# One list of 143 slot tiles for both parts of a grouped FFN, with its loads, prelude and last gathers rearranged

## The chip, the cores and the metric

The kernel runs on one core of a Trainium2 chip. The core has five engines with instruction streams of their own: TensorE (PE in the profile, with PEld for its weight loads), VectorE (DVE), ScalarE (ACT), GpSimd (POOL) and SyncE (SP, which issues transfers here). Sixteen DMA engines move data between HBM and the core's memory. The metric is the device time of one execution in microseconds (us); lower is better.

## The reference

Six residual blocks on 4096 tokens of width 256 (8 sequences of 512), each after a layer norm:

```python
x = x + 0.5 * L0_ffn(layernorm(x))     # 8 experts, each takes its best 1024 tokens, FF = 1024
x = x + L0_attn(layernorm(x))          # 16 heads of 16, rope, causal
x = x + 0.5 * L0_ffn(layernorm(x))
x = x + 0.5 * L1_ffn(layernorm(x))     # the grouped FFN of this case
x = x + L1_attn(layernorm(x))          # 16 heads of 64, no mask
x = x + 0.5 * L1_ffn(layernorm(x))     # the grouped FFN again, same weights
```

The block of this case routes every token to 4 of 16 experts and adds a shared expert:

```python
scores = softmax(xt @ gate_w.T)                     # 16 experts in 4 groups
gmask  = the 2 groups with the largest maximum
indices = top 4 of the masked scores; weights = scores at indices
a = silu(x @ w1[e]) * (x @ w3[e])                   # 256 -> 128 for each chosen expert e
y = sum over chosen e of weights[e] * (a @ w2[e])   # 128 -> 256
z = (silu(xt @ ws1) * (xt @ ws3)) @ ws2             # shared expert, inner width 256
return y + z
```

## The kernel before, in words

The residual x stays in the core's memory as 32 tiles of 128 tokens (`TT`). The blocks run one after the other: `ffn0(0)`, `attn0`, `ffn0(1)`, `ffn1_before` (the first grouped FFN), `attn1`, `ffn1_after` (the second). Inside the grouped FFNs every engine executes in the order in which the code is written; nothing is rearranged.

A grouped FFN works through lists in HBM. For each token and each of its four experts, `routing` computes a slot: a row in `slots_d`. The rows of one expert stand together and begin on a multiple of 128, so that a tile of 128 slots has one expert (`owner`). `send` scatters the normed rows of a token tile into their slots with four indirect DMAs from GpSimd (L1250). `tile_steps` then runs over the slot tiles, two at a time: `load` fetches a pair into one of four `xs` buffers from SP's queue (L1511), `turn` transposes it (tpx), `hide` multiplies with the expert's w1 and w3 (hs), `back` transposes the activations (tpa), and `give` multiplies with w2 (yps) and writes the result to `ys_d` (L1566). The stages of neighbouring pairs are interleaved: step i does `hide` of i - 2, `back` of i - 3, `turn` of i and `give` of i - 4. Slots that no token fills are zero rows; `clear` writes them once, in `ffn0(0)`.

`gather` brings the four result rows of each token of a tile back (L1357, four indirect DMAs from GpSimd, `yg` with two buffers), and `add` adds them to x on VectorE, weighted (L1370). `collect` makes a list of such steps: step t adds what step t - 2 gathered, and gathers for t. The number in `flying` says how many gathers may be under way: a gather waits for the one that many places before it. Sends have two under way.

The tokens are split in two parts with lists of their own (`PARTS`): 12 and 20 token tiles in the first grouped FFN, 20 and 12 in the second. A list for t token tiles must hold `slot_tiles(t)` slot tiles in the worst case, since each expert may leave one tile partly filled: 63 for 12 and 95 for 20. So part 0 can be sent and worked on while part 1 is still being routed, and part 0's results are gathered while part 1's tiles are in the loop.

- In `ffn1_before` the norms, logits and routing of part 0 come first, then its sends, then those of part 1, and beside them the shared expert's work as units in a `Pump` (`hidden` units with four matmuls, `outputs` units with two; while routing runs, the pump does one unit after every two or three steps of routing). After that come the 80 loop steps. From five steps after the last pair of part 0 one in three loop steps also does a step of `collect` for part 0. The weights of `attn1` (4 MB) are loaded from SP's queue at that point.
- In `attn1` part 1 is gathered in small pieces between the attention's work, and part 0 of the second FFN is normed, routed (`Front`) and sent.
- In `ffn1_after` part 1 is normed and its logits computed, then the loop starts; each of its first steps also does four steps of part 1's routing. Here two in three steps collect part 0 from the same point on. After the loop, 48 units of the shared expert run, and after every second unit one collecting step, first what is left of part 0 (two gathers under way), then part 1 (four).

`load(j)` is issued by `turn(j - 4)`, and each load waits for all sends of its part. Since SP works in order, a load that waits holds back the writes of `ys` behind it.

Of the kernel before, what the change touches and what calls it, by code (L numbers as in the profile page):

```python
# [19 lines left out]
P = 128  # L20
# [25 lines left out]
PARTS = 12, 20  # L46
# [9 lines left out]


def slot_tiles(t):

    return (t * P * TOPK + E1 * (P - 1)) // P  # L60


class Kernel:
    def __init__(self, ctx, tc, w):
# [59 lines left out]
        self.slots_d, self.ys_d = {}, {}  # L124
        for t in PARTS:
            self.slots_d[t] = self.dram.tile([slot_tiles(t) * P, D], F32, name=f"slots_d{t}")
            self.ys_d[t] = self.dram.tile([slot_tiles(t) * P, D], F32, name=f"ys_d{t}")

    def clear(self, zero, part, parts):

        for t in PARTS:
            rows = self.slots_d[t].rearrange("(j p) d -> p j d", p=P)
            a, b = slot_tiles(t) * part // parts, slot_tiles(t) * (part + 1) // parts
            self.nc.sync.dma_start(out=rows[:, a:b, :], in_=bc(zero, 1, b - a))
# [777 lines left out]
    def _attn1(self, ctx, weights, one, after):  # L912
# [191 lines left out]
        def listed(n):  # L1104
            b, c = divmod(n, NC)
            got = gathered(n - 1) if 1 <= n <= one.parts[1] + 2 else []
            if c == 0:
                ranges = []
                if b == 0:
                    ranges.append((self.stats1, QT, 2 * QT))  # L1110
                elif 2 <= b < B - 1:
                    got += [each(means, self.stats1, (b + 1) * QT + i) for i in range(0, QT, 2)]
                    ranges.append((self.stats1, (b + 1) * QT, QT))
# [106 lines left out]
class Grouped:  # L1220


    def __init__(self, k, n, parts):
        self.k, self.n, self.parts = k, n, parts
        self.base = (0, parts[0])
        self.tiles = [slot_tiles(t) for t in parts]
        self.slots_d = [k.slots_d[t] for t in parts]
        self.ys_d = [k.ys_d[t] for t in parts]
        late, most = k.late, max(parts)
# [4 lines left out]
        self.owner = [late.tile([1, slot_tiles(most)], I32, name=f"owner{h}") for h in range(2)]  # L1234
# [10 lines left out]
    def send(self, h, t, row):  # L1245

        nc, tc = self.k.nc, self.k.tc
        key = f"slots{self.n}{h}"
        for r in range(TOPK):
            inst = nc.gpsimd.indirect_dma_start(  # L1250
                out=self.slots_d[h][:, :],
                out_offset=bass.IndirectOffsetOnAxis(ap=self.slot[h][:, r, t : t + 1], axis=0),
                in_=row, in_offset=None,
                bounds_check=self.tiles[h] * P - 1, oob_is_err=True,
            ).ins
            before = self.sent[-2:-1]
            for other in before:
                tc.add_manual_dep(inst, other.name, SYNC, reason="two transfers at a time")
            tc.declare_no_dep(inst, group=key, keep=before, reason="slots of one part are all different")
# [4 lines left out]
    def routing(self, h, lg, pool, row_psum):  # L1264
# [49 lines left out]
        tiles_i = pool.tile([P, E1], I32, name="tiles_i")  # L1314
        nc.vector.tensor_scalar(tiles_i, inc[:, :, HT - 1], float(P - 1), None, ALU.add)
        nc.vector.tensor_scalar(tiles_i, tiles_i, 7, None, ALU.arith_shift_right)
        nc.vector.tensor_tensor(inc.rearrange(flat), inc.rearrange(flat), pb, ALU.subtract)
        pa = row_psum(E1 * HT)
        nc.tensor.matmul(pa, lhsT=k.tri, rhs=chosen.rearrange(flat), start=True, stop=True)
        tiles = pool.tile([P, E1], F32, name="tiles")  # L1320
        nc.vector.tensor_copy(tiles, tiles_i)
        upto = pool.tile([P, E1], F32, name="upto")
        nc.vector.tensor_tensor_scan(upto, k.ones[:, 0:E1], tiles, 0.0, ALU.mult, ALU.add)
        base = pool.tile([P, E1], F32, name="base")
        nc.vector.tensor_tensor(base, upto, tiles, ALU.subtract)
        nc.vector.tensor_scalar(base, base, float(P), None, ALU.mult)
        nc.vector.tensor_tensor(inc.rearrange(flat), inc.rearrange(flat), pa, ALU.add)
        yield
        nc.vector.tensor_tensor(inc, inc, bc(base, 2, HT), ALU.add)
# [11 lines left out]
        past = pool.tile([P, E1], F32, name="past")  # L1341
        number = pool.tile([P, 1], F32, name="number")
        nc.vector.tensor_scalar(past, upto, k.lanes[:, 0:1], None, ALU.is_le, ALU.add, accum_out=number)  # L1343
# [8 lines left out]
    def gather(self, h, t, flying):  # L1352

        nc, tc = self.k.nc, self.k.tc
        y = self.y[h, t] = self.k.late.tile([P, TOPK, D], F32, name="yg", bufs=2)
        for r in range(TOPK):
            inst = nc.gpsimd.indirect_dma_start(  # L1357
                out=y[:, r, :], out_offset=None, in_=self.ys_d[h][:, :],
                in_offset=bass.IndirectOffsetOnAxis(ap=self.slot[h][:, r, t : t + 1], axis=0),
                bounds_check=self.tiles[h] * P - 1, oob_is_err=True,  # L1360
            ).ins
            for other in self.got[-flying : 1 - flying]:
                tc.add_manual_dep(inst, other.name, SYNC, reason="few transfers at a time")
            self.got.append(inst)

    def add(self, h, t, ranks=range(TOPK)):
        at = self.base[h] + t
        x = self.k.x[:, at, :]
        for r in ranks:
            self.k.nc.vector.scalar_tensor_tensor(  # L1370
                x, self.y[h, t][:, r, :], self.coef[h][:, r, t : t + 1], x, ALU.mult, ALU.add
            )

    def collect(self, h, flying, then=None):

        def step(t):
            def run():
                if t >= 2:
                    self.add(h, t - 2)
                    if then is not None:  # L1380
                        then(self.base[h] + t - 2)
                if t < self.parts[h]:
                    self.gather(h, t, flying)
            return run
        return [step(t) for t in range(self.parts[h] + 2)]
# [66 lines left out]
    def shared(self, g):  # L1452
# [4 lines left out]
        def hidden(s):  # L1457
# [14 lines left out]

            def dve():
# [4 lines left out]
        def outputs(i):  # L1478
# [11 lines left out]

            def dve():
# [6 lines left out]
    def tile_steps(self):  # L1498
# [3 lines left out]
        where = [(h, i, min(2, self.tiles[h] - i)) for h in range(2) for i in range(0, self.tiles[h], 2)]  # L1502
        st = [{} for _ in where]

        def load(j):

            if j >= len(where):
# [3 lines left out]
            inst = nc.sync.dma_start(  # L1511
                out=st[j]["xs"][:, :n, :],
                in_=self.slots_d[h].rearrange("(j p) d -> p j d", p=P)[:, i : i + n, :],
            ).ins
            for other in self.of_part[h]:
                tc.add_manual_dep(inst, other.name, SYNC, reason="all rows of the part are there")

        def turn(j):
            h, i, n = where[j]
# [10 lines left out]
            load(j + 4)  # L1530
# [24 lines left out]
        def give(j):  # L1555
            h, i, n = where[j]
            yp = psum.tile([P, 2, D], F32, name="yps", tag="y", bufs=2)
            for u in range(n):
# [7 lines left out]
            nc.sync.dma_start(  # L1566
                out=self.ys_d[h].rearrange("(j p) d -> p j d", p=P)[:, i : i + n, :], in_=ys[:, :n, :]
            )
# [5 lines left out]

        first = sum(h == 0 for h, _, _ in where)
        return load, step, len(where) + 4, first


# [27 lines left out]


def ffn1_before(k, f):
# [3 lines left out]
    with ExitStack() as ctx, k.tc.manual_schedule(engines={E.PE, E.DVE, E.Activation, E.Pool, E.SP}):  # L1612
# [15 lines left out]
        f.logits(2, lg, 2 * QT)  # L1628
# [4 lines left out]
        pump.feed(groups[0][0] + groups[1][0] + groups[0][1] + groups[2][0])  # L1633
        steps = f.routing(0, lg, f.route, f.row_psum)
        pump.run(1)
        more = True
        while more:
            more = advance(steps, 3)
            pump.run(1)
        for t in range(a):  # L1640
            f.send(0, t, f.xn[:, t, :])
        load, step, total, first = f.tile_steps()
# [4 lines left out]
        k.ln_range(f.route, f.stats, a, 8)  # L1647
        pump.feed(groups[1][1] + groups[2][1])
        pump.run(2)
        f.normal(3)  # L1650
        f.normal(4)
        pump.run(2)
        f.columns(3)
        k.ln_range(f.route, f.stats, a + 8, TT - a - 8)
        pump.run(2)
        f.columns(4)
        f.logits(3, lg, 0)
        for g in range(5, 8):
            f.normal(g)
            pump.run(2)  # L1660
        pump.run(len(pump.units))
        f.logits(4, lg, QT)
        pump.feed(groups[3][0])
        for g in range(5, 8):
            f.columns(g)
            pump.run(1)
            f.logits(g, lg, (g - 3) * QT)
        pump.feed(groups[4][0] + groups[3][1])
        for g in range(5, 8):
# [245 lines left out]
```

## Time and profile before

| | |
|---|---|
| timed runs | 4051.42 us median of three (4050.55 to 4054.75) |
| profiled execution | 4017.39 us, span 4015.7 us, mean granted TensorE clock 0.936 |
| busy in the span | PE 3662.2 us (91%), DVE 1858.5 (46%), ACT 1432.8 (36%), POOL 1203.8 (30%) |
| first grouped FFN | x is back at 1859.06 us, first slot tile transposed at 2029.18, attention's first transposes at 2310.58 |
| second grouped FFN | first norm operation at 3560.73, first slot tile transposed at 3581.12, first gather of part 0 at 3763.31, last gather at 3980.06 |

The profile shows one execution on the core. "Busy" is the time in which an engine executes instructions; a wait is given with what ended it. A group "yg<-ys_d" is the instructions that write the tile yg from ys_d, and "L1357" is the line that issued them. Times within the span are counted from its start.

### The profile page before, as it was taken

What the parts mean: (1) busy time and instruction counts of PE and PEld (TensorE: products, weight loads), DVE (VectorE), ACT (ScalarE), POOL (GpSimd) and SP (SyncE); (2) the same over time, 40 slices, a digit from 0 to 9 for tenths busy, and PEclk for the clock granted to TensorE, in tenths of its full rate; (3) what the DMA queues carried; (4) which work ended last, traced back from release to release, by engine and by line L of the source; (5) the groups of instructions that cost most, each with busy time, mean ns of one, the idle gap of its engine ahead of it and who ended that gap; (6) DMA issues with size and microseconds to landing.
All of it is one profiled execution on the core that took longest, in us unless ns stands there. A gap on an engine that the chain in (4) does not pass through costs nothing.

```text
span 4015.7 us, 52125 instructions
## 1 busy us (share of the span) xinstructions
PE 3662.2 (91%) x18444; PEld 2343.5 (58%) x18444; DVE 1858.5 (46%) x4396; ACT 1432.8 (36%) x2849; POOL 1203.8 (30%) x1074
## 2 busy tenths in 40 slices
PE   5799995999997599997798999999999999989978
PEld 5466662555556366665487845555555554558855
DVE  5312206555553421213733556666556576554444
ACT  2122221444443122222122355555455554533311
POOL 2233335334322133331553322220000004504254
PEclk6899997999986599998899999999999999989989
DMA  8533322010103033324256600110000001136543
GB/s 271 161 73 75 73 30 80 17 27 17 28 22 106 18 77 71 70 52 123 78 198 218 188 28 27 30 29 1 1 1 1 1 1 48 58 108 218 182 147 105
DMA packets 256141, 306.99 MB, mean 76 GB/s; under 512 B 34320, under 2 KB 225936, under 8 KB 255632
## 3 DMA queue, kind: packets, MB, share of 16 engines
q1 hardware_dynamic: 206736, 202.43, 15.8%
q0 software_dynamic: 49152, 101.24, 10.5%
q8 instruction: 153, 2.51, 0.3%
q14 instruction: 100, 0.82, 0.1%
HBM read 161.48 MB, written 133.69 MB: 74 GB/s over the span
## 4 chain that ended last, share of the span: by engine, by line
PE 41%; issue 4%; DVE 3%; DMA 3%; POOL 3%; ACT 1%; POOLq 0%; DVEq 0%; ACTq 0%; SPq 0%
PE sp L986 6%; PE tp L1006 6%; PE zp L1033 6%; PE pq L964 6%; PE hs L1537 4%; PE yp L1048 3%; PE pv L953 3%; PE yps L1559 2%; POOL slots_d L1250 2%; DMA yg<-ys_d,slot 2%; PE hp L1464 2%; POOL yg L1357 1%; PE tpx L1523 1%; DMA acc_d<-ob,idx 1%; PE rp L1020 1%
## 5 line engine op out<-in xcount | busy, mean ns | idle before, releaser
L478 PE MATMUL hp<-exT,w 128*128 128x512 f32 x1024 | 453.4, 597 | 0.0
L492 PE MATMUL op<-w,hid 128*128 128x256 f32 x2048 | 451.9, 380 | 0.0
L995 ACT ACTIVATE ex<-sp,nmax 128x512 f32<-128x512 f32 x512 | 344.7, 685 | 242.3 <-DVE nmax L992 242.3
L492 PEld LDWEIGHTS op<-w,hid 128*128 128x128 f32 x2048 | 387.7, 190 | 64.3 <-issue 15.3
L1357 POOL DMA_INDIRECT yg<-ys_d,slot x256 | 266.0, 1039 | 510.2 <-DVE x L1370 296.2
L497 DVE TENSOR_TENSOR ob<-op,b 128x256 f32<-128x256 f32 x128 | 54.4, 425 | 647.4 <-PE op L492 572.0
L731 DVE CUSTOM_DVE_ANT_0 junk<-sp,mask 128x128 f32<-128x128 f32 (+3 forms) x512 | 251.1, 490 | 198.0 <-PE sp L722 174.3
L499 POOL DMA_INDIRECT acc_d<-ob,idx x128 | 207.1, 1618 | 439.8 <-ACT ob L498 193.0
L992 DVE TENSOR_REDUCE nmax<-sp 128x2 f32<-128x1024 f32 x256 | 301.7, 1220 | 80.3 <-PE sp L986 80.2
L478 PEld LDWEIGHTS hp<-exT,w 128*128 128x128 f32 x1024 | 193.5, 191 | 219.9 <-issue 216.9
L1006 PEld LDWEIGHTS tp<-ident,ex 128*128 128x128 f32 x2048 | 234.4, 141 | 147.4 <-issue 86.6
L1537 PE MATMUL hs<-w_sb,xT 128*128 x1264 | 310.4, 390 | 2.5 <-DMA xs<-slots_d 1.3
L482 ACT ACTIVATE hid<-hp,b 128x512 f32<-128x512 f32 x256 | 175.9, 687 | 342.3 <-PE hp L478 342.3
L1006 PE MATMUL tp<-ident,ex 128*128 128x128 f32 x2048 | 272.5, 275 | 6.7 <-ACT ex L995 5.4
L1537 PEld LDWEIGHTS hs<-w_sb,xT 128*128 128x128 f32 x1264 | 248.4, 197 | 39.2 <-ACT xT L195 2.7
L1250 POOL DMA_INDIRECT slots_d<-wide,slot x176 | 174.4, 991 | 318.3 <-DVE past L1343 144.3
L986 PE MATMUL sp<-qk,qk 64*128 64x512 f32 x1024 | 254.4, 615 | 0.0
L964 PE MATMUL pq<-xnT,wide 128*128 128x512 f32 x512 | 247.5, 607 | 1.2 <-ACT xnT L195 0.8
L197 DVE COPY eT<-tp 128x512 f32<-128x512 f32 x256 | 176.9, 691 | 140.7 <-PE tp L1006 139.9
L1033 PE MATMUL zp<-eT,v 128*64 128x512 f32 x1024 | 236.0, 603 | 0.0
L195 ACT COPY eT<-tp 128x512 f32<-128x512 f32 x256 | 149.5, 584 | 240.4 <-PE tp L1006 240.4
L449 POOL DMA_INDIRECT ex<-xn_d,idx x128 | 131.3, 1025 | 345.9 <-DVE idx L440 311.8
(298 smaller groups left out, 5512.3 us busy)
## 6 DMA issues: line engine op xcount, KB each, us to landing
xs<-slots_d SPq DMA_DIRECT2D x156, 256.0 KB, 2.8
ys_d<-ys SPq DMA_DIRECT2D x156, 256.0 KB, 2.5
w<-in_W SPq DMA_DIRECT2D x32, 1024.0 KB, 6.1
w_sb<-in_w SPq DMA_DIRECT2D x24, 512.0 KB, 6.5
slots_d<-zero SPq DMA_DIRECT2D x7, 1536.0 KB, 12.9
xn_d<-xn SPq DMA_DIRECT2D x16, 512.0 KB, 4.2
acc_d<-x SPq DMA_DIRECT2D x8, 1024.0 KB, 5.7
x<-acc_d SPq DMA_DIRECT2D x8, 1024.0 KB, 9.5
```

Of the source, the lines that this page charges most:

```text
L478: nc.tensor.matmul(hp, lhsT=w1[:, c, f * P : f * P + P], rhs=exT[e][:, c, h * CH : h * CH + CH], start=(c == 0), stop=(c == DC - 1),)
L492: nc.tensor.matmul(op, lhsT=hid[h][:, f, i * P : i * P + P], rhs=w2[:, f, :], start=(f == 0), stop=(f == FC - 1),)
L731: nc.vector.tensor_tensor_reduce(out=junk[:, :wd], in0=sps[h // 2][:, h % 2, at : at + wd], in1=mask[:, S - wd :], scale=1.0, scalar=NEG, ...
L964: nc.tensor.matmul(pp, lhsT=(wq, wk)[a][:, k, c * P : c * P + P], rhs=xnT[b][:, k, :], start=(k == 0), stop=(k == DC - 1),)
L986: nc.tensor.matmul(sp[:, j, :], lhsT=q[r, qt * P : qt * P + P], rhs=k[r, :], start=True, stop=True)
L992: nc.vector.tensor_reduce(nmax, sp, AX.X, ALU.max, negate=True)
L995: nc.scalar.activation(ex[:, j, :], sp[:, j, :], AF.Exp, bias=nmax[:, j : j + 1], accum_out=ch["sums"][:, qt, j : j + 1],)
L1006: nc.tensor.transpose(tp[:, k, :], ch["ex", qt][:, j, k * P : k * P + P], self.ident)
L1033: nc.tensor.matmul(zp[DK1 * j : DK1 * j + DK1, :], lhsT=v[b, h][:, k, at : at + DK1], rhs=ch["eT"][:, j, k, :], start=(k == 0), stop=(k == ...
L1250: inst = nc.gpsimd.indirect_dma_start(out=self.slots_d[h][:, :], out_offset=bass.IndirectOffsetOnAxis(ap=self.slot[h][:, r, t : t + 1], ax ...
L1357: inst = nc.gpsimd.indirect_dma_start(out=y[:, r, :], out_offset=None, in_=self.ys_d[h][:, :], in_offset=bass.IndirectOffsetOnAxis(ap=self ...
L1537: nc.tensor.matmul(hp[:, u].rearrange("p a i -> p (a i)"), lhsT=st[j]["xT"][:, u, c, :], rhs=self.w13[:, bass.ds(st[j]["e"][u], 1), c, :]. ...
```

## The change

Both parts now share one list. Part 0 fills whole tiles from the front: of the rows of an expert, those that make full tiles go to that expert's tiles (`upto`), and the rest, fewer than 128, go to one tile per expert behind them (`tail`), which part 1 completes before it opens new tiles. In all there are `SLOT_TILES` = 143 tiles. The first 4a - 16 of them (a token tiles in part 0) are full for certain once part 0 is sent, so they are what `tile_steps` calls the tiles of h = 0: 48 in the first FFN, whose parts are now 16 and 16, and 64 in the second (20 and 12). All others (95 and 79) wait for both parts. Part 0's results stand in the first 4a + 16 tiles (`whole`), and its gathers may start when those are written: 40 and 48 pairs (`known`).

- The loads of the tiles of h = 1 are issued when the loop reaches them, four at once and then one ahead by four as before; in the last four steps of h = 0 nothing is loaded.
- Sends have four under way instead of two.
- In `ffn1_before` the norms, columns and logits of part 1 become steps of a generator, followed by its routing, and `Pump.beside` runs units beside both routings: three steps for a hidden unit, one for an output unit, four when there is no unit.
- Collecting beside the loop: three in five steps in both FFNs (before: one in three, two in three). In `ffn1_after` routing takes three steps per loop step instead of four.
- After the loop of `ffn1_after` the collecting steps that are left are spread evenly over the units, and part 1 is gathered four token tiles deep: every second tile uses two `xs` buffers in place of a `yg`.

```diff
-PARTS = 12, 20
+PARTS = (16, 16), (20, 12)
+SLOT_TILES = (NT * TOPK + E1 * (P - 1)) // P
...
     def clear(self, zero, part, parts):
-        for t in PARTS:
-            rows = self.slots_d[t].rearrange("(j p) d -> p j d", p=P)
...
+        rows = self.slots_d.rearrange("(j p) d -> p j d", p=P)
+        a, b = SLOT_TILES * part // parts, SLOT_TILES * (part + 1) // parts
+        self.nc.sync.dma_start(out=rows[:, a:b, :], in_=bc(zero, 1, b - a))
...
+        first = TOPK * parts[0] - E1
+        self.starts, self.tiles = (0, first), (first, SLOT_TILES - first)
+        self.whole = TOPK * parts[0] + E1
...
     def send(self, h, t, row):
-            before = self.sent[-2:-1]
+            before = self.sent[-4:-3]
...
     def routing(self, h, lg, pool, row_psum):
+        if h == 0:
+            nc.vector.tensor_copy(tiles_i, count)
+            nc.vector.tensor_scalar(tiles_i, tiles_i, 7, None, ALU.arith_shift_right)
...
+            nc.vector.tensor_tensor(jump, tail, at, ALU.subtract)
...
+        nc.vector.scalar_tensor_tensor(beyond, inc, 0.0, bc(jump, 2, HT), ALU.is_ge, ALU.mult)
+        yield
+        nc.vector.tensor_tensor(inc, inc, bc(at, 2, HT), ALU.add)
+        nc.vector.tensor_tensor(inc, inc, beyond, ALU.add)
...
-    def gather(self, h, t, flying):
+    def gather(self, h, t, flying, more=False):
+        if more and t % 2:
+            halves = [self.work.tile([P, 2, D], F32, name="xs", bufs=4) for _ in range(2)]
+            y = [halves[r // 2][:, r % 2, :] for r in range(TOPK)]
...
-    def collect(self, h, flying, then=None):
+    def collect(self, h, flying, then=None, more=False):
+        depth = 4 if more else 2
...
         def turn(j):
+            if j == early:
+                for ahead in range(4):
+                    load(j + ahead)
...
-            load(j + 4)
+            if j >= early or j + 4 < early:
+                load(j + 4)
...
+    def beside(self, steps):
+        more = True
+        while more:
+            more = advance(steps, self.units[0][0].steps if self.units else 4)
+            self.run(1)
...
 def ffn1_before(k, f):
+        def second():
+            for g in range(a // QT, TT // QT):
+                for i in range(0, QT, 2):
+                    for t in range(g * QT + i, g * QT + i + 2):
+                        k.ln_mean(f.route, f.stats, t)
+                    yield
+                y = k.ln_root(f.route, f.stats, g * QT, QT)
+                yield
+                k.ln_rest(f.route, f.stats, g * QT, QT, y)
+                yield
+                f.normal(g)
+                yield
+                f.columns(g)
+                f.logits(g, lg, g * QT - a)
+                pump.feed(groups[g][0])
...
+            yield from f.routing(1, lg, f.route, f.row_psum)
+        pump.beside(second())
...
-        begin, weights = first + 5, None
+        begin, weights = known + 5, None
...
-            if i >= begin and (i - begin) % 3 == 0 and coming:
+            if i >= begin and (i - begin) % 5 % 2 == 0 and coming:
...
 def ffn1_after(k, f, out):
-        begin = first + 5
+        begin = known + 5
...
-                sending = not advance(steps, 4)
+                sending = not advance(steps, 3)
...
-            if i >= begin and (i - begin) % 3 != 2 and early:
+            if i >= begin and (i - begin) % 5 % 2 == 0 and early:
...
-        last = f.collect(1, 4, done)
+        last = f.collect(1, 4, done, more=True)
...
+        ends = early + last
+        pace, at = len(ends) / len(pump.units), 0
         while pump.units or pump.pending:
             pump.run(1)
             at += 1
-            if at % 2 == 0 and early:
-                early.pop(0)()
-            elif at % 2 == 0 and last:
-                last.pop(0)()
+            if ends and len(early + last) - len(ends) < at * pace:
+                ends.pop(0)()
```

In `turn`, `early` is the number of pairs of h = 0 (24 and 32).

## The prediction

> **What bounds the kernel now.** I read the slices first, to find the stages that this change touches, then busy time by stretch inside them, then GpSimd's timeline and the waits. TensorE is busy 91% of the span, and the attention stage from 2310 to 3560 us is at nine tenths or more almost everywhere. The two grouped FFNs stand at 1859 to 2310 us and 3560 to 4016 us, and there it is not one engine.
>
> ```profile
> 2040.00:2060.00 20.00, 20.00 (x114) 17.85 (x113) 7.74 (x16) 7.03 (x17) 10.86 (x12) 1.00 0.69 232
> 2120.00:2140.00 20.00, 11.78 (x63) 9.92 (x61) 4.85 (x10) 3.60 (x9) 9.30 (x10) 0.84 0.42 138
> 2160.00:2180.00 20.00, 15.06 (x80) 12.91 (x78) 5.87 (x12) 4.77 (x12) 5.05 (x5) 0.95 1.02 363
> 3700.00:3720.00 20.00, 20.00 (x112) 17.81 (x111) 7.68 (x16) 6.76 (x16) 0.00 (x0) 1.00 0.48 159
> 3820.00:3840.00 20.00, 16.80 (x76) 14.08 (x75) 8.21 (x18) 4.86 (x11) 11.56 (x11) 0.83 0.60 180
> 3960.00:3980.00 20.00, 15.97 (x45) 9.34 (x45) 9.50 (x21) 2.36 (x4) 15.49 (x15) 0.83 0.52 149
> ```
>
> Columns: stretch, then busy us of PE, PEld, DVE, ACT, POOL, then clock granted, DMA share, GB/s. The tile loop runs TensorE full (first and fourth row). It has holes where the first FFN passes from part 0 to part 1 (second row) and while the attention weights load (third). From 3763 us on TensorE is no longer full although the loop goes on until 3902: GpSimd's timeline says why.
>
> ```profile
> 3763.31 1.07 POOL L1357 DMA_INDIRECT yg<-ys_d,slot  x1 [65.78 <-DMA ys_d<-ys]
> ...
> 3779.44 1.02 POOL L1357 DMA_INDIRECT yg<-ys_d,slot  x1 [1.95 <-DVE as L1545]
> 3780.76 1.14 POOL L1357 DMA_INDIRECT yg<-ys_d,slot  x1 [0.30 <-issue]
> 3783.21 1.02 POOL L1357 DMA_INDIRECT yg<-ys_d,slot  x1 [1.31 <-DMA yg<-ys_d,slot]
> 3785.26 1.02 POOL L1357 DMA_INDIRECT yg<-ys_d,slot  x1 [1.03 <-DMA yg<-ys_d,slot]
> ...
> 3906.57 1.02 POOL L1357 DMA_INDIRECT yg<-ys_d,slot  x1 [1.20 <-DVE x L1370]
> ...
> 3912.48 1.21 POOL L1357 DMA_INDIRECT yg<-ys_d,slot  x1 [1.63 <-DMA yg<-ys_d,slot]
> ...
> 3980.06 1.02 POOL L1357 DMA_INDIRECT yg<-ys_d,slot  x1 [0.31 <-issue]
> ```
>
> A gather step is four of these. With two in flight each pair waits for the pair before: 17 steps from 3779.44 to 3906.57 are 7.48 us each. The last 48 gathers, four in flight, run from 3912.48 to 3981: 1.33 us each where nothing stops them, GpSimd's own pace. VectorE adds a step's rows two steps later, in order with the copies that TensorE needs, so a late gather stops TensorE.
>
> **The change, part by part** (profiled execution 4017.39 us, span 4015.7; the median of the timed runs is 4051.42, 34 us above it. I take the difference in us and put it on the median.)
>
> *Fewer tiles.* 63 + 95 slot tiles per FFN become 143. A full loop step (two tiles) is 3.247 us in the chain of waits (the hs pieces at 3632.12 and 3635.37), so 15 tiles are 24.4 us of TensorE per FFN, 49 in both. This is the gain only where TensorE ends last, so each stage is worked out by what ends it.
>
> *Zero fill.* 15 tiles x 128 KB = 2.0 MB less. The fill holds the DMA at 1.0 from 62 to about 136 us, at some 345 GB/s: 5.7 us shorter. The first ex gathers are issued at 123.82 and paced by GpSimd at 1.3 us; the first landed 7.2 us later where 2.8 is the least seen, but the eighth, issued at 133.3, is what counts. I take -1 (0 to -3).
>
> *Prelude of the first FFN.* Part 0 now has 16 token tiles. Logits are ready at about 1886 instead of 1882.2. Routing took 34.4 us to its slot list (1882.2 to 1916.6), 8.7 of them waits; with 16 tiles (VectorE operations of 256 elements, not 192: some 35 x 0.06), 2.5 us of new operations and four more shared units between, I get 42, so slots at 1928. Then 64 sends. Before they were 48 in 68 us (1.4 each, two in flight); with four in flight GpSimd's 0.98 + 0.30 decides: 64 x 1.31 = 84, to 2012, landing 2.4, load 2.9: first transposes at 2018 instead of 2029.18. Routing of part 1 runs beside this stream and should be done by 2008 to 2018, so it is covered; if it is late, it is what starts the sends of part 1. The 27 us of shared units that stood between that routing and the loop before (2002 to 2029) are now inside. -11 (-16 to +2).
>
> A rule weighed here: the built order has 13 table loads on ScalarE in this prelude, 8 before, since square roots now alternate with Silu for each group.
>
> ```profile
> 1886.42 1.28 ACT L1275 ACT_TABLE_LOAD   x1
> 1887.71 0.36 ACT L1275 ACTIVATE score<-score 128x192 f32<-128x192 f32 x1
> ```
>
> The activation starts 0.01 us after the load has ended, so five more are 6.4 us. The Trainium skill, "ScalarE: Activation LUTs", section "What ACT_TABLE_LOAD costs", adds a drain of 1.38 us to the 1.28 and comes to 2.66 for a switch: 13.3 us. That speaks against the change. By either figure routing of part 1 ends near the 2018 that the sends set; I use the row.
>
> *Loop of the first FFN.* Part 0 is now 24 steps: at 2018 + 4 (ramp) + 78 = 2100 the loads of part 1 are issued, when it begins and not four steps ahead. Its 64 sends take 84 us from 2012: they are in at about 2099. So of the hole in the second row (8.2 us) 2.5 stay: a load lands after 2.8 to 2.9 us, of which the step's two other stages hide about one; the writes of ys queued behind it on SP are needed by nobody then. The weights' hole (5 us) stays. The first gather waits for tile pair 40, steps 43 plus 4 us: 2167. Two steps beside the 4 MB of weights took 19.5 us before; with the wait for their additions 21. Then 14 more. They are asked for in three of five loop steps, every 5.4 us of TensorE's time, and take 7.46: TensorE, which would be done at 2275, waits. 2167 + 21 + 14 x 7.46 + 2.4 + 4 = 2299, against 2306.8. So with the prelude's gain the first FFN gives -8, not -24 (-18 to +3).
>
> *Attention.* Four gather steps fewer for part 1; it is TensorE's stage, so nothing. Routing for the second FFN has some 2.5 us more VectorE work, at a place where TensorE already stood (13.3 busy of 20 us at 3340): +1 (0 to +3).
>
> *Second FFN to its first gather.* Same prelude. Part 0's tiles in the list reach 32 steps, but the gathers still need 48 pairs. The boundary at step 32 shows 2.5 us that were hidden before; routing asks three steps of each loop step, not four, and has 3 us more to do: +2. Sends start at about 3626, 48 x 1.31 = 63, in by 3691, wanted at 3701. First gather 3763.3 + 4.5.
>
> *From the first gather to the end.* 252.4 us before. Now 23 loop steps follow, with 14 gather steps at 5.4 us of TensorE's pace: again gathers decide, 14 x 7.46 = 104.4. Six more come beside the shared units, without loads and writes; the attention stage shows 6.1 (2328.64 to 2334.78), I take 6.5: 39, landing 2.4. Until then VectorE has let 15 of 48 units pass (one collecting step for every two units). The other 33 took 2.26 each before (44 units from 3912.5 to 4012.1): 74.6, and 3.6 from the last matmul to the end. The last 48 gathers, 63.6 us with two buffers more, run beside them and end earlier. 224 against 252.4: -28 (-38 to -15).
>
> Costed at nothing: the marks and owner operations (VectorE, inside the routing figures), the statistics moved between loop and attention (0.6 us of VectorE per tile, in a stage that TensorE bounds), pool sizes. Without cover the routing's additions would be 3 us each.
>
> Sum: -1 - 8 + 1 + 4.5 - 28 = -31.5, so 4020.
>
> **The rivals.** (1) Sends not helped by four in flight. Beside the loop they took 1.61 (first FFN) and 1.73 us (second). DMA share there was 0.7 of which loads and writes are 0.48, so the engines have room, which speaks against. If so, the boundaries wait: 64 x 1.61 = 103 from 2012 makes +15, 48 x 1.73 = 83 makes +10: about 4045. (2) Gathers keep up: at the 6.1 of the quiet stage, 14 steps x 1.36 in each loop, 19 twice: about 3985. Against it stands 7.48 over 17 steps beside the same loads and writes. (3) Slower: gathers in the loop become costlier, since they now share the tail with denser asking, and VectorE, in order, stops TensorE for each. Every us on 28 steps is 28 us; from 8.6 us a step the gain is gone. Only beside the weights did a step take 9.7; at 9 it is 28 x 1.5 = 42, about 4062. (4) That tiles do not go away is excluded: the built program has 180 matmuls fewer.
>
> **How the numbers follow.** Likeliest, 4020: 0.60. Rival 1: 0.16, rival 2: 0.11, rival 3: 0.10, something else slower 0.03. A measurement of this kernel tells about 0.2% (8 us). Faster holds the first three but for a little of each: 0.82; same 0.06; slower 0.12. The range, 3990 to 4048, takes in the likeliest with its bounds, most of rival 2 and rival 1, and leaves out rival 3.
>
> **What would show it.** First transposes of slot tiles near 2018; loads of part 1 issued right after the last send; the first FFN ending near 2299 with TensorE below 18 of 20 us over its last 120 us and "DVE x <- DMA yg" in the waits; the same from 3767 to about 3872; GpSimd's last gather before 3985; at the end units back to back. It is wrong if gather steps in the loops are far from 7.5 us, if a hole over 8 us stands at step 24 or 32, or if the attention stage is longer by more than 3 us.

## The result, and the profile after

The changed kernel takes 4205.74 us (median of 4 runs, 4201.69 to 4210.15) against 4051.41 us beside it: a ratio of 1.038, 95% interval 1.0362 to 1.0398. It is 154 us slower, where I forecast 31.5 us faster. Its profiled execution has a span of 4200.0 us.

First the busy time by stretch, as before (columns: stretch, then busy us of PE, PEld, DVE, ACT, POOL, then clock granted, DMA share, GB/s):

```profile
1940.00:1960.00 20.00, 6.09 (x20) 4.86 (x20) 0.00 (x0) 0.60 (x1) 15.26 (x16) 0.59 0.30 103
1980.00:2000.00 20.00, 5.38 (x15) 4.00 (x16) 3.06 (x11) 0.00 (x0) 15.31 (x16) 0.50 0.30 104
2040.00:2060.00 20.00, 18.13 (x63) 10.64 (x62) 11.65 (x36) 7.13 (x9) 0.00 (x0) 0.91 0.00 0
2120.00:2140.00 20.00, 3.78 (x8) 2.52 (x8) 0.00 (x0) 0.58 (x1) 15.29 (x16) 0.59 0.35 117
2180.00:2200.00 20.00, 20.00 (x108) 17.62 (x108) 6.60 (x14) 6.58 (x15) 0.00 (x0) 0.96 0.50 158
3780.00:3800.00 20.00, 0.00 (x0) 0.00 (x0) 0.69 (x1) 0.00 (x0) 15.35 (x16) 0.50 0.34 118
```

Four rows have GpSimd at 15.3 of 20 us with 16 transfers. In them TensorE, VectorE and ScalarE stand most of the time, and the DMA is at 0.3, so it isn't full. In the two rows where GpSimd rests the others work. The three stretches of standing (about 1936 to 2013, 2096 to 2178 and 3765 to 3815) are the three streams of sends. GpSimd's timeline in the first one:

```profile
1962.07 0.99 POOL L1245 DMA_INDIRECT slots_d<-wide,slot  x1 [0.30 <-issue]
1963.36 0.98 POOL L1245 DMA_INDIRECT slots_d<-wide,slot  x1 [0.30 <-issue]
...
2086.58 0.98 POOL L1245 DMA_INDIRECT slots_d<-wide,slot  x1 [80.99 <-DVE slot L1367]
```

A send every 1.29 us, each with 0.30 us of "issue" ahead: GpSimd never waits for a transfer. That is the pace that I forecast. The sends of part 1 come late (2086.58) because VectorE, which routes part 1 in that time, stands. VectorE's timeline, then TensorE's:

```profile
1962.61 0.42 DVE L1547 SCALAR_TENSOR_TENSOR x<-yp,x 128x256 f32<-128x256 f32 x1 [25.41 <-remote]
...
1973.81 0.42 DVE L1547 SCALAR_TENSOR_TENSOR x<-yp,x 128x256 f32<-128x256 f32 x1 [9.70 <-remote]
...
1985.01 0.42 DVE L1547 SCALAR_TENSOR_TENSOR x<-yp,x 128x256 f32<-128x256 f32 x1 [10.70 <-issue]
```

```profile
1963.09 2.08 PE L1539 MATMUL yp<-ws_sb,at 128*128 128x256 f32 x4 [17.00 <-issue]
1974.29 2.08 PE L1539 MATMUL yp<-ws_sb,at 128*128 128x256 f32 x4 [9.12 <-issue]
1985.49 2.08 PE L1539 MATMUL yp<-ws_sb,at 128*128 128x256 f32 x4 [9.12 <-issue]
```

TensorE ends four matmuls at 1965.17, and the VectorE instruction that waits for TensorE's semaphore alone starts at 1973.81, 8.64 us later. 0.48 us after its start TensorE begins the next four, and again it takes 8.64 us until VectorE knows. "remote" stands where the semaphore that ended the wait was raised at that moment, but the instruction that raises it had ended long before. Here it is TensorE's semaphore. So TensorE's report to the other engines is late. I count as late every recorded rise of TensorE's semaphore over 1 us after the end of the last matmul that raises it (this trace records 3382 rises for 3499 such matmuls). In this trace such rises stand inside the streams of sends and behind the last gathers (from 4120 us), the worst 30.5 us. VectorE's and ScalarE's semaphores have none before the very end of the span. The profile of before has none but at the very end of its span.

A second thing differs in the two traces. The table of DMA issues of before gave landing times for nearly every line; that of after gives none:

```profile
xs<-slots_d SPq DMA_DIRECT2D x142, 256.0 KB
```

Of the 12288 landings that 768 GpSimd transfers leave (16 each) the trace of before holds 12282, that of after 6981. And before's profiled execution, 4017.39 us, was 34 us faster than its timed runs. Both come back in the experiments.

### The profile page after: what moved, and what is told of

Its sections match the earlier page's. It is cut to its first block, busy times and chain, and to the rows that moved or that the text cites. A ratio compares the mean times of both kernels' runs of the same rounds, so it can differ in the third digit from the quotient of the medians.

```text
span 4200.0 us, 51261 instructions
## 1 busy us (share of the span) xinstructions
PE 3653.2 (87%) x18174; PEld 2315.6 (55%) x18174; DVE 1846.2 (44%) x4410; ACT 1422.8 (34%) x2815; POOL 1206.9 (29%) x1074
## 4 chain that ended last, share of the span: by engine, by line
PE 73%; issue 8%; DVE 6%; DMA 5%; another core or an unknown queue 5%; POOL 2%; ACT 2%; SPq 0%; POOLq 0%; DVEq 0%; ACTq 0%
PE hp L471 10%; PE op L485 10%; PE sp L979 6%; PE pq L957 5%; PE tp L999 5%; PE zp L1026 5%; PE hs L1602 4%; PE yp L1041 3%; PE pv L946 3%; DMA yg<-ys_d,slot 2%; PE hp L1515 2%; PE st L760 2%; PE yps L1624 2%; PE sp L715 2%
## 5 line engine op out<-in xcount | busy, mean ns | idle before, releaser
L1402 POOL DMA_INDIRECT yg<-ys_d,slot x232 | 242.4, 1045 | 654.6 <-DMA ys_d<-ys 283.9
L485 PEld LDWEIGHTS op<-w,hid 128*128 128x128 f32 x2048 | 386.9, 190 | 65.1 <-issue 15.3
L1602 PE MATMUL hs<-w_sb,xT 128*128 x1144 | 291.5, 400 | 25.0 <-issue 9.0
L1602 PEld LDWEIGHTS hs<-w_sb,xT 128*128 128x128 f32 x1144 | 231.4, 203 | 64.4 <-issue 11.6
```

Of the source, the lines that this page charges most:

```text
L485: nc.tensor.matmul(op, lhsT=hid[h][:, f, i * P : i * P + P], rhs=w2[:, f, :], start=(f == 0), stop=(f == FC - 1),)
L1402: inst = nc.gpsimd.indirect_dma_start(out=y[r], out_offset=None, in_=self.k.ys_d[:rows, :], in_offset=bass.IndirectOffsetOnAxis(ap=self.sl ...
L1602: nc.tensor.matmul(hp[:, u].rearrange("p a i -> p (a i)"), lhsT=st[j]["xT"][:, u, c, :], rhs=self.w13[:, bass.ds(st[j]["e"][u], 1), c, :]. ...
```

## The experiments

Theory A: an unbroken stream of GpSimd's transfers makes TensorE's reports late. Theory B: the order is at fault (part 1 routed too late, its loads behind its last send).

**The number in flight, in both kernels, and a pause.** In send():

```diff
-            before = self.sent[-4:-3]
+            before = self.sent[-2:-1]      # e1_two; e4_three has [-3:-2]
```

> The changed kernel with its sends two in flight again, nothing else. Theory A (a stream of sends that never waits for a transfer delays what TensorE reports to ScalarE and VectorE): the sends take 1.40 us each or more, the holes of 60 to 80 us in TensorE during the three bursts of sends go, time 4020 to 4080. Theory B (the order is at fault: part 1 is routed too late and its loads wait for its last send, whatever the pace): 128 sends at 1.4 instead of 1.29 us are 14 us longer, time 4190 to 4230.

> The changed kernel with three sends in flight. A send lands some 2.25 us after its issue and one is issued every 1.29 us, so a wait for the third one back is always over: theory A expects the time of the changed kernel, 4190 to 4215. If the number allowed in flight counts by itself, it lies between two and four: 4080 to 4170. Theory B: 4200.

The kernel before with [-4:-3] in place of [-2:-1], and nothing else:

> The kernel before with its sends four in flight, nothing else. Theory A: 1.29 us a send, and TensorE, ScalarE and VectorE stand in each burst; slower than before by 60 to 150 us (4110 to 4200). Theory B: sends end 0.1 to 0.3 us each earlier, time 4035 to 4055.

The changed kernel, four in flight, with this behind every four sends (pause is a tile of 128 x 32 that nobody else reads):

```diff
+        nc.gpsimd.memset(self.pause, 0.0)
+        for _ in range(4):
+            nc.gpsimd.tensor_scalar(self.pause, self.pause, 1.0, None, ALU.add)
```

> The changed kernel, four in flight, with a memset and four small tensor_scalar operations of GpSimd after every four sends, some 1 us in which it issues no transfer. Theory A in the form that the gaps count: as with two in flight, 4020 to 4090. Theory A in the form that a wait for a transfer has to be between sends: as the changed kernel, 4190 to 4240. Theory B: 4200 to 4240.

Measured, before at 4050.92: two in flight 4105.33 us (ratio 1.0132, 1.0110 to 1.0154), three 4203.89 (1.0372, 1.0344 to 1.0400), before with four 4194.66 (1.0349, 1.0314 to 1.0384), the pause 4068.55 (1.0041, 1.0023 to 1.0059). Theory B falls: one subscript makes the kernel before 144 us slower, with its list, prelude and loads untouched. Its trace stands in the same way in its own streams:

```profile
1960.00:1980.00 20.00, 2.44 (x10) 2.43 (x10) 0.00 (x0) 1.17 (x2) 13.50 (x14) 0.50 0.28 99
2100.00:2120.00 20.00, 3.09 (x7) 1.46 (x5) 0.42 (x1) 0.00 (x0) 15.43 (x16) 0.50 0.29 105
```

The pause takes 137 us off the changed kernel while it makes each stream longer (1.77 us a send). Two in flight helped less than I expected: beside the loop its sends wait and take 1.63 us, without late reports, but in the prelude, where little else uses the DMA (its share is 0.28 from 1940 to 2000 us, against 0.68 from 2100 to 2160), they take 1.36 us and TensorE reports up to 25.5 us late. Three in flight gave the stream of four, 1.29 us a send, and the same time. So the number allowed in flight counts here as far as it makes GpSimd wait.

**A second trace of before, and a memset that made no gap.** The kernel before was run unchanged for a trace. Three kernels got one memset behind every second transfer (`if r % 2: nc.gpsimd.memset(self.pause, 0.0)`): the changed one in its sends; the same also in its last gathers; before in its last gathers.

> The kernel before, unchanged, to get a second trace of it: its profiled execution of 4017.39 us was 34 us below the median of its own timed runs. Theory A: the timed runs hold stalls of the same kind that this one profile lacked, so a new trace shows a span near 4049 and reports of TensorE over 1 us late in the last 48 gathers, which run at 1.33 us each with no wait between. The other theory (the 34 us lie outside the span): span 4016 again, 34 us below its time, no late reports.

> The changed kernel, four sends in flight, with one small memset of GpSimd after every second send only. Theory A, gaps count: some 0.3 us in 2.6 are enough, no late reports while it sends, the streams of 64 sends take 90 to 95 us where the long pause took 118, so 20 to 50 us less than with the long pause: 4020 to 4050. If a gap has to be as long as a transfer's landing: stalls as in the changed kernel, 4150 to 4210.

> The same, with the memset also after every second of the last gathers, which are four deep. Theory A: the late reports of the last 60 us go too, 15 to 35 us less than with the memset in the sends alone: 3990 to 4030, faster than the kernel before. If the last gathers are limited by their own pace: 2 to 6 us more than with the memset in the sends alone.

> The kernel before with one small memset of GpSimd after every second of its last 48 gathers. Theory A: its own stalls at the end go and it takes 4015 to 4030. The other theory: 48 gathers take 4 to 8 us longer, beside TensorE, 4048 to 4060.

The new trace of before: span 4057.4 us, not 4015.7, and late reports of up to 21.9 us in its first sends and of up to 5.5 us at its last gathers. Two of its stretches, and behind them the first one in the first profile:

```profile
1960.00:1980.00 20.00, 2.82 (x22) 2.43 (x22) 0.69 (x1) 1.18 (x2) 14.48 (x16) 0.58 0.27 96
3980.00:4000.00 20.00, 9.12 (x18) 4.93 (x19) 3.62 (x9) 1.77 (x3) 11.76 (x12) 0.51 0.35 97
```

```profile
1960.00:1980.00 20.00, 17.67 (x60) 9.89 (x59) 12.78 (x35) 5.42 (x8) 14.05 (x15) 0.91 0.26 93
```

The first slot tiles come 27 us later than in the first profile (2056.5 against 2029.2). So the kernel before holds stalls of this kind too, by the difference of the times some 34 us of its 4051 (its first profile had 4017), and the profile from which I forecast was of an execution without them. The three memsets failed as experiments of a gap: 4203.82, 4206.25 and 4051.69 us, nothing changed. GpSimd's timeline says why:

```profile
1927.17 0.99 POOL L1246 DMA_INDIRECT slots_d<-wide,slot  x1 [0.18 <-issue]
1928.46 0.98 POOL L1246 DMA_INDIRECT slots_d<-wide,slot  x1 [0.30 <-issue]
1929.44 0.13 POOL L1261 MEMSET pause<- 128x16 f32 x1
1929.75 0.98 POOL L1246 DMA_INDIRECT slots_d<-wide,slot  x1 [0.18 <-issue]
```

The memset runs inside the 0.30 us that lie between two transfers anyway; the next send still starts 1.29 us after the one ahead, as in 113 of the 127 steps of this FFN's sends. In most of the others the memset itself stood, so that the mean is 1.37 to 1.40 us:

```profile
1994.86 0.11 POOL L1261 MEMSET pause<- 128x16 f32 x1 [1.20 <-remote]
```

It waits only for GpSimd's own semaphore, for the memset before, and that too rose late, by up to 4.1 us in these two runs of the changed kernel. So the lateness is not TensorE's alone. As controls the three are of use: another GpSimd operation between the transfers takes no stall away if it leaves most of their pace.

**Real gaps.** The same helper with two tensor_scalar operations in place of four, which wait for each other:

> The changed kernel, four in flight, with a real gap in GpSimd's stream: a memset and two tensor_scalar operations that wait for each other, some 1.0 us, after every four sends and after every four of the last gathers. (The memset alone of two runs before started inside the 0.30 us that lie between two transfers anyway, and left the pace at 1.29 us: those two made no gap.) Theory A: no late reports in sends or last gathers; streams of 64 sends in 98 us instead of 118; first FFN 25 us and the end 20 us less than with the long pause in the sends alone: 4010 to 4045. If it is the last gathers' own pace (1.6 us now) that bounds the end: 4060 to 4080.

> The kernel before with the same gaps in its sends (two in flight) and in its last 48 gathers. Theory A: its own stalls (16 us of TensorE at 1960 to 1980 and about 15 at 3980 to 4000 in its second trace) go: 4015 to 4040, the time of its first profile. Otherwise its sends only get longer: 4055 to 4075.

> The changed kernel with the 1.0 us gap after every four sends only. Theory A: as with gaps in both, plus the late reports of the last gathers, 15 to 30 us: 4030 to 4065.

```profile
1934.71 0.99 POOL L1252 DMA_INDIRECT slots_d<-wide,slot  x1 [0.30 <-issue]
1935.69 0.17 POOL L1243 MEMSET pause<- 128x32 f32 x1
1935.95 0.88 POOL L1245 TENSOR_SCALAR pause<-pause 128x32 f32<-128x32 f32 x2
1937.07 1.05 POOL L1252 DMA_INDIRECT slots_d<-wide,slot  x1 [0.24 <-issue]
```

That is GpSimd's timeline of the changed kernel with these gaps: from 1934.71 to 1937.07 are 2.36 us, 1.07 more than 1.29. Before at 4052.37: the changed kernel with gaps takes 4032.31 us (ratio 0.9952, 0.9940 to 0.9965), before with gaps 4039.10 (0.9968, 0.9949 to 0.9987), gaps in the sends alone 4040.13 (0.9971, 0.9951 to 0.9990). All three expectations of theory A held. Where there is a gap, no report inside a stream is over 1.2 us late; where the last gathers have none, 12.4 and 12.0 us late ones stand there.

With gaps in both, the changed kernel is 7 us ahead, not 31.5 (timed; 11 in the profiled executions). The traces, stage by stage, changed minus before: first FFN's last slot-tile matmul +14 us (2329.3 against 2315.1), attention +2, on to the first gather +6, from the first gather to the end -34 (232.6 against 266.9). The loss stands in the first FFN. Its slot tiles begin 7 us later (2029.9 against 2022.9), and at its first boundary, where the longer stream of sends ends at 2125, a hole of 22 us (before with gaps has one of 19) holds back the first gather, which now waits for 40 pairs (2199.8 against 2161.5). The hole:

```profile
2080.00:2100.00 20.00, 20.00 (x112) 17.77 (x112) 7.58 (x17) 6.84 (x16) 15.17 (x23) 1.00 0.73 232
2100.00:2120.00 20.00, 8.34 (x46) 7.16 (x44) 3.52 (x7) 2.85 (x7) 15.08 (x24) 0.77 0.36 125
2120.00:2140.00 20.00, 9.27 (x41) 7.77 (x42) 2.30 (x5) 2.13 (x5) 5.30 (x9) 0.63 0.42 136
```

**How much gap, and what the parts are worth.** One tensor_scalar less; the gap after every eight sends only (`if t % 2:`); last gathers with two buffers (`f.collect(1, 4, done)`); two in flight with the gap.

> Gaps as in the run with gaps in both, but one tensor_scalar less: about 0.65 us after every four transfers, a send every 1.45 us. If this is still gap enough: no late reports, the stream of 128 sends is 14 us shorter and with it the hole at the boundary of the first FFN (22 us there): 4012 to 4026. If the gap is too short: late reports again, 4060 to 4200.

> The 1.0 us gap after every eight sends, and after every four of the last gathers as before: a send every 1.42 us. If the share of the gap decides (it is 9% here, 11% with the shorter gap after every four): no late reports, 4010 to 4026. If a queue fills within a few sends and each needs its own gap: late reports in the sends, 4060 to 4200.

> The run with gaps in both, but with the last gathers' two buffers of before instead of four. If the gain of 34 us behind the first gather comes from the order (fewer loop steps, one gather step for every so many units): within 8 us of that run, 4028 to 4042. If it comes from the depth: 4050 to 4066.

> The run with gaps in both, but with two sends in flight. Before, sends beside the loop took 1.61 us with two in flight; with the gap they take 1.57 with four. If four in flight is worth anything: its stream beside the loop becomes 1.75 to 1.85 us a send and the holes grow, 4040 to 4065. If the gap stands in for the wait: within 6 us, 4027 to 4039.

Before at 4049.35: 4029.88 us (0.9948, 0.9931 to 0.9964), 4095.49 (1.0107, 1.0085 to 1.0130), 4031.53 (0.9950, 0.9931 to 0.9970) and 4058.34 (1.0022, 1.0011 to 1.0033). Over the runs of the changed kernel in which it shows, the lateness falls as the stream gets slower:

| sends of the first FFN | mean us a send | latest report of TensorE in the sends of either FFN | time |
|---|---|---|---|
| unbroken (4 in flight, 3) | 1.29 | 31 us | 4206, 4204 |
| memset behind every second | 1.37 to 1.40, most of them 1.29 | 29 us | 4204, 4206 |
| two in flight, prelude | 1.36 | 25.5 us | 4105 |
| 1.0 us after every eight | 1.42 | 5.6 us | 4095 |
| 0.65 us after every four | 1.49 | 1.7 us | 4030 |
| 1.0 us after every four | 1.58 | 1.1 to 1.5 us | 4032 (gathers without gaps: 4040) |
| 1.8 us after every four | 1.77 | none over 1 us | 4069 |

With the 0.65 us gap the hole at the boundary is gone, but only because the loop comes there later: reports are 1 to 1.75 us late beside it, TensorE is busy 55.7 of the 70 us from 2040 (68.3 with the 1.0 us gap), and step 24 begins at 2132.9 against 2130.4. My 4012 to 4026 was missed by 4 us. The depth of the last gathers is worth nothing, so the 34 us come from the rest of what changed there (fewer loop steps behind the first gather, collecting spread over the units); no run parts these. Four in flight is worth about 26 us (4058.34 against 4032.31, from two sets of runs), but only with the gap. A gap doesn't stand in for the wait; the two add up to 1.72 us a send and a hole of 36 us.

**Where nothing stalls.** Before with four in flight and the 1.0 us gaps, and the changed kernel with gaps only where they had shown a need (1.0 us beside the loops and in the last gathers, 0.65 in the prelude, none in attention):

> The kernel before with its sends four in flight and the 1.0 us gaps in sends and last gathers. If four in flight with gaps is what helps: the 80 sends beside its loop take 1.57 us each, its hole at the first boundary falls from 18 us to 5 or less, 4020 to 4032, level with the changed kernel with gaps. If the tile list and the order carry the changed kernel's lead: within 6 us of two in flight with gaps, 4033 to 4045.

> The changed kernel with the 1.0 us gap after every four sends beside the loops and every four of the last gathers, 0.65 us in the prelude of the first FFN, none in the attention stage. Theory A: no late reports, the stream of 128 sends 6 us shorter and the attention stage as without gaps: 4018 to 4032. If the attention stage needs them too, or the prelude does: late reports there and over 4036.

4018.13 and 4022.27 us, but the unchanged kernel before took 4020.07 in this set of runs where it had taken 4049 to 4052 in every earlier one: ratios 0.9996 (0.9987 to 1.0006) and 1.0003 (0.9991 to 1.0015). The traces of this set hold 12279 and 12269 of the 12288 landings; all those of the earlier experiments hold 7076 to 9252. These two runs can't be laid beside the earlier ones, and the question that they were made for stays open. They raised another one, for the last run: the changed kernel as it is.

> The changed kernel, unchanged. If the kernel before takes about 4050 beside it: 4200 to 4210 again. If the kernel before takes about 4020 beside it and the stalls are absent there: no late reports, and my sum applies, 31.5 us below before (3975 to 4010), a ratio of 0.990 to 0.998. If the changed kernel's unbroken stream stalls even there: 4100 to 4210, a ratio over 1.02.

3992.43 us against 4017.13: a ratio of 0.9940, 0.9921 to 0.9960. The same program that lost 154 us wins 25. Its stream of sends is nearly as unbroken as in its first trace (first fence, GpSimd; 121 of 127 steps take 1.3 us, there 125), and VectorE follows TensorE at once (second fence; four matmuls that end at 1937.82 are known to it at 1937.86). The third has the busy time by stretch:

```profile
1959.62 0.98 POOL L1245 DMA_INDIRECT slots_d<-wide,slot  x1 [0.30 <-issue]
1960.91 0.98 POOL L1245 DMA_INDIRECT slots_d<-wide,slot  x1 [0.31 <-issue]
```

```profile
1937.86 0.42 DVE L1547 SCALAR_TENSOR_TENSOR x<-yp,x 128x256 f32<-128x256 f32 x1 [3.12 <-PE yp L1539]
...
1939.57 0.43 DVE L1547 SCALAR_TENSOR_TENSOR x<-yp,x 128x256 f32<-128x256 f32 x1 [0.21 <-PE yp L1539]
```

```profile
1960.00:1980.00 20.00, 17.73 (x70) 11.21 (x69) 6.34 (x19) 7.81 (x11) 15.38 (x16) 0.84 0.30 103
2080.00:2100.00 20.00, 15.24 (x84) 13.28 (x82) 6.05 (x12) 5.17 (x13) 15.07 (x16) 1.00 0.54 181
2100.00:2120.00 20.00, 15.73 (x69) 13.21 (x70) 4.61 (x9) 3.76 (x8) 0.00 (x0) 0.74 0.47 150
```

And its table of DMA issues has the landing times again (last column, median us):

```profile
xs<-slots_d SPq DMA_DIRECT2D x142, 256.0 KB, 2.9
```

## Why the prediction was wrong, and where it was right

The trace of the last run is the one to lay beside the profile that I forecast from: neither has stalls in the sends. Step by step, against before's 4015.7:

| step | forecast | last run |
|---|---|---|
| first transposes of slot tiles | 2018 | 2018.3 (before 2029.2) |
| send, us each (mean) | 1.31 | 1.30 in part 0, 1.31 in part 1 |
| sends of part 1 begin | 2012, or 2018 if routing is late | 2016.3 |
| hole at step 24 | 2.5 us | 8.8 us |
| first gather | 2167 | 2174.8 |
| first transposes of attention, against before | -8 | -0.4 (2310.2) |
| attention | +1 | +0.4 |
| on to the first gather of the second FFN | +4.5 | +2.3 |
| from there to the end | 224 us, -28 | 221.9 us, -30.5 |
| span | -31.5 | -28.2 (3987.5) |

The prelude and the end are right to 3 us. In between, the routing of part 1 was late: GpSimd waited 12.63 us for VectorE's slot list before its first send of part 1. I had counted that routing as covered or, at worst, done by 2018, but carried the sum on with 2012. The hole at step 24 is 6 us larger (12.06 us from one step's transposes to the next, less 3.25): the sends begin 4.3 us later than in the sum, and the loop is ready for that step at 2095, not at 2100. A hole over 8 us there is one of the signs of being wrong that the forecast named. The step behind it takes another 3.7 us, for which the sum had no term. The first gather is 8 us late, and the gathers hand the delay on (first two steps 24.2 us where I had 21, then 7.80 us a step, not 7.46): attention's first transposes wait 6.05 us for what VectorE does behind its last additions. The loop's gain became nothing, and nearly all that the last run wins is won behind the first gather of the second FFN. The three waits:

```profile
2016.30 0.98 POOL L1245 DMA_INDIRECT slots_d<-wide,slot  x1 [12.63 <-DVE slot L1367]
2103.89 1.12 PE L1587 MATMUL tpx<-ident,xs 128*128 128x128 f32 x4 [8.66 <-DMA xs<-slots_d]
2310.16 1.12 PE L938 MATMUL tpn<-ident,xn 128*128 128x128 f32 x3 [6.05 <-DVE xn L923]
```

The rule on table loads: the sends of part 1 began at 2016.3, inside my 2008 to 2018, which were made with the trace's 1.28 us a load. That alone would not refute the larger figure, but in this trace too, where nothing else held it up, the activation follows a load's end within 0.02 us.

The 4205.74 us came from two steps.

First, "with four in flight GpSimd's 0.98 + 0.30 decides". The pace was right, 1.29 us in every unbroken run. What I costed at nothing, without naming a cover, was what a GpSimd that never waits does to the engines beside it. That was neither a step nor a rival: my slow case was dearer gathers at 4062, with something else slower at 0.03. What the runs showed in its place: TensorE's reports come up to 31 us late, and one subscript that takes the wait out of the kernel before costs it 144 us. The two traces of the changed kernel, the same program, tell where its time went: with the stalls the first slot tile comes 71 us later (2089.7 against 2018.3), the first FFN's last slot-tile matmul ends 137 us later (2440.9 against 2304.1), the first gather of the second FFN starts 189 us later (3954.9 against 3765.6), and the span is 212 us longer (4200.0 against 3987.5).

Second, the line on the 34 us between before's profile and its median: "I take the difference in us and put it on the median". The second trace shows them to be stalls of the very kind that the change multiplies, in the sends at 1960 to 1980 and in the last gathers. A profile that is 0.8% faster than every timed run of its kernel lacks something that the runs have, and a sum made on it can't see what an edit does to that. The forecast should have kept a case for it.

What is shown: in the sets of runs that have stalls, taking the waits out of the stream brings more of them, in either kernel, and a gap of 1 us after every four sends takes them away but for reports up to 1.5 us late; in the last set the same stream does no harm. What stays open: where in the chip the reports are held up, and why some sets of runs have it and others not. All traces with late reports before the very end of the span lack landing records (6981 to 8607 of 12288 are there), and the traces with 12265 to 12282 have no such report. But the loss of records is not what the stalls leave behind: before with gaps has 8890 landings, two in flight with gaps 9252, and neither has a late report before the very end; and the first trace of the changed kernel has only 894 of 1312 landings in its first 400 us, long before its first late report. So the missing records mark the set of runs, and within such a set the pace of the stream decides. The number of the chip does not tell the sets apart: the record has 0 for the first four experiments, which stall, and 0 for the last run, which does not. No run tests whether the chip or the recording makes the difference; a span and a granted clock are on record for each timed run too, so none of them is known to have run unrecorded.

As to what to use: with gaps after every four transfers the changed kernel is faster than both where the stalls are (4032.31 against 4052.37, ratio 0.9952; its own time without gaps was 4205.74). Where they are not, it is fastest as it stands (0.9940); a variant with gaps is level with before there (1.0003).

## What to carry to other kernels

Compare the profiled execution's own time with the timed runs before you build a sum on it; if it is faster than all of them, take a second trace first. When an edit takes the last wait out of a stream of GpSimd transfers, ask what the other engines do meanwhile, and try a short gap in the stream, checking in the timeline that it moved the pace. Where TensorE, VectorE and ScalarE stand together and one busy engine is left, look for waits that end long after the instruction waited for, and change that engine's pace alone, in the old kernel too: one subscript there separated the cause from the rest of a large change.

## What was not expected of the hardware

In most sets of runs an unbroken stream of GpSimd's indirect transfers (0.98 us busy and 0.30 between, 0.3 of the DMA's time) made TensorE's semaphore rise up to 31 us late; 8.64 us came three times in a row. Before the very end of the span ScalarE's had no late rise in any run, VectorE's two (1.9 and 1.2 us, before with four in flight), while GpSimd's own, where the memsets let one see it, came up to 4.1 us late. The lateness fades between 1.36 and 1.58 us a send, not at one point. The last gathers at 1.33 us do it too, less (up to 13 us). Three and four transfers allowed in flight made no difference, since neither makes GpSimd wait. And the same program lost 154 us in one set of runs and gained 25 in another.
